# Scatters to expert slots issued from a list, two or three a round, with a fixed GpSimd order, in layer 3's cross attention

## The chip, the cores and the metric

The kernel runs on one core of a Trainium2 chip. A core has five engines that run side by side, each with a queue of instructions of its own which it takes in order: TensorE (PE, matrix products and transposes), VectorE (DVE), ScalarE (ACT), GpSimd (POOL) and SyncE (SP, here only DMA issue). An instruction waits for the work of other engines by semaphores, and whatever stands behind it on its own engine waits too. GpSimd does arithmetic and also issues DMAs, among them the indirect ones that are the subject here.

The metric is the device time of one execution in microseconds (us), less is better.

## The reference

The reference is a decoder of four layers on `x` of 4 batches x 512 tokens x 128 features; each layer adds self attention, cross attention to a context of 77 rows, and a feed-forward part to `x`. What matters here is the end, layer 3's cross attention and its feed-forward part, a mixture of 32 experts with a limited number of slots each:

```python
# cross attention: 16 heads of 64, 77 keys
scores = jnp.einsum('bhqd,bhkd->bhqk', q, k) * scale
attn = jax.nn.softmax(scores, axis=-1)
out = jnp.einsum('bhqk,bhkd->bhqd', attn, v)
...
# feed-forward: every token goes to K = 4 of E = 32 experts, C = 128 slots an expert
scores = jax.nn.sigmoid(logits)
_, idx = jax.lax.top_k(scores + bias[None, :], K)
w = jnp.take_along_axis(scores, idx, axis=-1)
w = w / jnp.clip(jnp.sum(w, axis=-1, keepdims=True), 1e-12, None)
pos = jnp.take_along_axis(jnp.cumsum(onehot, axis=0) - 1, eid[:, None], axis=1)[:, 0]
valid = pos < C
xe = jnp.zeros((E, C, D), x.dtype).at[eid, posc].add(jnp.where(valid[:, None], Xrep, jnp.zeros((), x.dtype)))
h = jax.nn.silu(jnp.einsum('ecd,edi->eci', xe, W1)) * jnp.einsum('ecd,edi->eci', xe, W3)
ye = jnp.einsum('eci,eid->ecd', h, W2)
out = (ye[eid, posc] * gflat[:, None]).reshape(-1, K, D).sum(axis=1)
out = out + jax.nn.silu(X @ sw1.T) * (X @ sw3.T) @ sw2.T
```

A token's slot within an expert is its place in the count over all earlier tokens, so batches are routed one after the other.

## The kernel before

**Rounds of the cross attention.** `l3_xattn` goes through 32 items: four batches of eight pairs of heads. `lagged` makes rounds of four phases: in round r it writes the projection of item r, the scores and softmax of item r-1, the product with the values (`acc`) of item r-4, and the transposes (`turn`) of item r-3. The scores are two score tiles an item; for each, VectorE takes the maximum, subtracts it, ScalarE takes the exponential, VectorE sums and takes the reciprocal, and GpSimd multiplies by it (the multiplication at L2165, tile `heads`). TensorE's transposes of `heads` (L2173) need both multiplications of their item.

**The routing beside it.** When the last item of a batch is summed (`yT`, L2188), `chain5` adds it to `x`, normalizes the tokens and calls `route_slots`: router matmuls, sigmoid, top four, the running counts, and for each token and choice the number of its slot (`to`) and its row with weight and place (`sent`, last written at L784). Then 16 indirect DMAs (L788; four tiles of tokens by four choices, 128 rows each) scatter the rows into the tensor `slots`. GpSimd issues them. Batches 0, 1 and 2 go this way; batch 3 is computed densely at the end, from bf16 copies of the weights (`in_bf16`, six loads that GpSimd issues since they cast).

**Order.** `weave(dense, chain, every)` runs the generator `dense` and takes one step of `chain` for each `every` steps of it; what is left of the chain follows at the end. The first 40 steps of the rounds have the norms of other batches beside them, the next 32 have batch 0's routing, the next 32 batch 1's, and the rest batch 2's. What is written so isn't yet the order of the queues: a scheduler takes the instructions by priority and by its own estimate of when they are ready, and orders every engine's queue. Under `manual_schedule` an engine keeps the order in which its instructions were written; before, only VectorE does so, in the last part. `alone` declares that scatters needn't wait for each other.

**After the rounds.** `slot_experts` fetches the slots of four experts at a time (SP, L837), which needs all scatters done, turns them on TensorE (L842), multiplies with the experts' weights and scatters the results back (L885). `returned` adds them to `x` and stores it. Shared rows and the dense path of batch 3 are woven with it.

The names that the prediction speaks of: `heads` L2165 and L2173, `slots` L788, `sent` L784, `yT` L2188, `kb` (the keys, cleared at L2112), and the loads at L375.

Of the kernel before, what the change touches and what calls it, by code (L numbers as in the profile page):

```python
# [23 lines left out]
B, S, D = 4, 512, 128  # L24
# [14 lines left out]
class Pack:  # L39


    def __init__(self):
        self.parts, self.at, self.n = [], {}, 0
# [248 lines left out]
class Net:  # L292
# [7 lines left out]
    def __init__(self, ctx, tc, packs, dram, feed):  # L300
        self.tc, self.nc = tc, tc.nc
        self.packs, self.dram = packs, dram
        self.feed, self.loaded = feed, []
        self.stay = {}
        self.turn = 0
        self.last = []
        self.chunks, self.sums = {}, {}
        nc = self.nc
        pool = lambda name, bufs, **kw: ctx.enter_context(tc.tile_pool(name=name, bufs=bufs, **kw))
        self.keep = pool("keep", 1)  # L310
        self.wpool = pool("weights", self.SLOTS)
        self.small = pool("small", 4)
        self.away = pool("away", 1, space=bass.MemoryType.DRAM)

        k = self.keep
        self.x = k.tile([P, NT, D], F32, name="x")
        self.xn = k.tile([P, NT, D], F32, name="xn")
        self.xT = k.tile([P, NT * P], F32, name="xT")
        xin = dram["x"].rearrange("(t p) d -> p t d", p=P)
        fetch = lambda b: nc.sync.dma_start(self.x[:, TB * b : TB * b + TB, :], xin[:, TB * b : TB * b + TB, :])  # L320
        fetch(0)
        self.want(0)
        self.const = self.load("const", k, "const")
        self.want(1)
        for b in range(1, B):
            fetch(b)
        self.ident = k.tile([P, P], F32, name="ident")
        make_identity(nc, self.ident)
        self.ones = k.tile([P, P], F32, name="ones")
        nc.gpsimd.memset(self.ones, 1.0)  # L330
        self.identb = k.tile([P, P], BF16, name="identb")
        nc.vector.tensor_copy(self.identb, self.ident)
        self.onesb = k.tile([3, P], BF16, name="onesb")
        nc.gpsimd.memset(self.onesb, 1.0)

        self.causal = k.tile([P, P], BF16, name="causal")
        nc.gpsimd.memset(self.causal, 0.0)
        nc.gpsimd.affine_select(
            out=self.causal, in_=self.causal, pattern=[[-1, P]], compare_op=ALU.is_ge,
            fill=-BIG, base=0, channel_multiplier=1,  # L340
        )
# [3 lines left out]
    def pool(self, name, bufs=1, right=False):  # L345
        return self.tc.tile_pool(
            name=name, bufs=bufs, side="right" if right else "left", reuse_waits="tile"
        )
# [400 lines left out]
    def route_slots(self, b, W, pool):  # L749


        nc = self.nc
        E, K = 32, 4
        m = {}
        one = lambda shape, name: pool.tile(shape, F32, tag=name, name=name, bufs=1)
        own = lambda shape, dt, name: pool.tile(shape, dt, name=f"{name}{b}", bufs=1)
        yield from self.capped(b, W, pool, m)

        code = one([P, TB, E], "code")
        self.tt(code, m["place"], self.const["slot1"].unsqueeze(1).to_broadcast([P, TB, E]), ALU.add)  # L760
        self.tt(code, code, m["fits"], ALU.mult)
        yield
        m8 = one([P, TB, 8], "m8")
        for t in range(TB):
            nc.vector.max(m8[:, t, :], code[:, t, :])
        yield
        top = m8[:, :, :K]
        to, none = own([P, TB, K], I32, "to"), one([P, TB, K], "none")
        nc.vector.tensor_scalar(none, top, 0.0, 2.0 * E * CAP, ALU.is_equal, ALU.mult)
        nc.vector.scalar_tensor_tensor(to, top, -1.0, none, ALU.add, ALU.add)  # L770

        sent = pool.tile([P, TB, K, D + 2], F32, name="sent", tag="sent", bufs=2)
        for t in range(TB):
            nc.scalar.copy(sent[:, t, :, :D], self.xn[:, TB * b + t, :].unsqueeze(1).to_broadcast([P, K, D]))
        nc.vector.tensor_scalar(
            sent[:, :, :, D + 1].bitcast(I32), self.const["place"].rearrange("p (t k) -> p t k", k=K),
            float(b * S * K), None, ALU.add,
        )
        yield
        same = one([P, TB, K, E], "same")  # L780
        wide = lambda a: a.unsqueeze(2).to_broadcast([P, TB, K, E])
        self.tt(same, wide(code), top.unsqueeze(3).to_broadcast([P, TB, K, E]), ALU.is_equal)
        self.tt(same, same, wide(m["w"]), ALU.mult)
        nc.vector.tensor_reduce(sent[:, :, :, D], same, AX.X, ALU.add)  # L784
        for t in range(TB):
            for k in range(K):

                self.alone("slots", nc.gpsimd.indirect_dma_start(  # L788
                    out=self.slots, out_offset=bass.IndirectOffsetOnAxis(ap=to[:, t, k : k + 1], axis=0),
                    in_=sent[:, t, k, :], in_offset=None, bounds_check=E * CAP - 1, oob_is_err=False,  # L790
                ))
                if k % 2:
                    yield

    def alone(self, group, put):

# [1322 lines left out]
    def l3_xattn(self, base, pool):  # L2119
# [3 lines left out]
        nc, tc = self.nc, self.tc  # L2123
# [18 lines left out]
        def scores(b, hp):  # L2142
            q = made.pop((b, hp, "q"))
            es = []
            for j0 in range(0, TB, 2):
                s = self.mm((P, 4, L))
                for j in range(2):
                    self.dot(
                        s[:, 2 * j : 2 * j + 2, :].rearrange("p h l -> p (h l)"),
                        (q[:, (j0 + j) * P : (j0 + j + 1) * P], kb[:, hp, b].rearrange("p h l -> p (h l)")),  # L2150
                    )
                es.append(s)
            if hp == 0:
                made[b, "e"] = pool.tile([P, TB, 16, L], F32, tag="heads", name="heads", bufs=2)
            for i, s in enumerate(es):
                s = s.rearrange("p (j h) l -> p j h l", j=2)
                e = made[b, "e"][:, 2 * i : 2 * i + 2, 2 * hp : 2 * hp + 2, :]
                m, r = (pool.tile([P, 2, 2], F32, tag=t, name=t, bufs=8) for t in ("sm_m", "sm_s"))
                wide = lambda a: a.unsqueeze(3).to_broadcast([P, 2, 2, L])
                nc.vector.tensor_reduce(m, s, AX.X, ALU.max)  # L2160
                self.tt(e, s, wide(m), ALU.subtract)
                nc.scalar.activation(e, e, AF.Exp)
                nc.vector.tensor_reduce(r, e, AX.X, ALU.add)
                nc.vector.reciprocal(r, r)
                nc.gpsimd.tensor_tensor(e, e, wide(r), ALU.mult)  # L2165

        def turn(b, hp):
            e = made[b, "e"].rearrange("p j h l -> p j (h l)")
            for i in blocks[hp]:
                r0, r1 = rows[i]  # L2170
                t = self.mm((P, TB, P))
                for j in range(TB):
                    nc.tensor.transpose(t[: r1 - r0, j, :], e[:, j, r0:r1], self.ident)  # L2173
                eT = pool.tile([P, S], F32, tag="eT", name="eT", bufs=4)
                nc.scalar.copy(eT[: r1 - r0], t[: r1 - r0].rearrange("l j q -> l (j q)"))
                made[b, i] = eT

        def values(b, hp):
# [7 lines left out]
            if hp == HP - 1:  # L2186
                self.sums["l3_xattn", b] = pool.tile([P, S], F32, tag="yT", name="yT", bufs=2)
                nc.scalar.copy(self.sums["l3_xattn", b], accs[b])  # L2188

        return self.lagged(items, (projections, 0), (scores, 1), (values, 4), (turn, 3))  # L2190

    def out(self, b):
# [5 lines left out]
def chained(*chains):  # L2198
    for c in chains:
        yield from c  # L2200


def some(steps, n):

    for _ in range(n):
        if next(steps, steps) is steps:
            return
        yield


def build(nc, packs, dram):
# [4 lines left out]
    at = {}  # L2216
# [6 lines left out]
    with tile.TileContext(nc) as tc, ExitStack() as ctx:  # L2223
        net = Net(ctx, tc, packs, dram, feed)
# [118 lines left out]
        steps = net.l3_xattn(at["x3"], x3)  # L2343
# [5 lines left out]
        def onto_x3(b):  # L2349
            net.add_columns(b, net.sums.pop(("l3_xattn", b)))  # L2350
            yield
            yield from net.norm(b)
# [2 lines left out]
        W5 = Both()  # L2355
        chain5 = lambda b: chained(onto_x3(b), net.route_slots(b, W5, s5))
        net.weave(some(steps, 40), chained(net.norm(1), net.norm(2), net.norm(3)), 3)
        net.weave(some(steps, 32), chain5(0), 1.35)
        net.want(at["l3"] + 1)
        net.weave(some(steps, 32), chain5(1), 1.35)  # L2360
        net.weave(steps, chain5(2), 1.0)
        net.add_columns(3, net.sums.pop(("l3_xattn", 3)))
        close_pool("x3")
        close_pool("x3c")
# [43 lines left out]
```

## Time and profile before

| | us |
|---|---|
| three runs | 2242.82, 2245.49, 2256.26 |
| median | 2245.49 |
| the profiled execution | 2248.78 |
| its span in the trace | 2247.0 |
| mean granted TensorE clock | 0.958 of full |

The trace is of the profiled execution, so sums of its durations stand against 2248.78 and 2247.0, not against the median.

A row of a group of instructions reads: line, engine, operation, what is written <- what is read (buffer numbers left out), shape, count | busy time, mean ns of one | idle time of the engine just ahead of them, and what ended most of it. A row of a timeline reads: start, duration, engine, line, operation, and in brackets the idle time ahead of it and what ended that. Where the stage lies, in times from the span's start:

| event | us |
|---|---|
| first multiplication of `heads` on GpSimd | 1984.78 |
| sums `yT` of batches 0, 1, 2, 3 copied | 2015.56, 2049.10, 2095.98, 2141.48 |
| first scatter of batches 0, 1, 2 | 2047.71, 2093.93, 2138.26 |
| last scatter begins | 2157.58 |
| slots fetched, first issue | 2159.73 |
| first scatter back | 2179.67 |

One scatter takes GpSimd 966 to 1132 ns (median 972), and lands a median 2.1 us after its issue.

### The profile page before, as it was taken

The numbers are of one execution on the slowest core, as the hardware profiler recorded it, in microseconds if no ns is written. First come the engines' busy times: TensorE is split into PE (matmuls) and PEld (weight loads), VectorE is DVE, ScalarE is ACT, GpSimd is POOL, SyncE is SP. The second block draws the span as 40 slices with busy tenths as digits, with TensorE's granted clock in tenths as the row PEclk, the third lists the DMA queues.
The fourth block names the chain that finished last, engine by engine and source line by source line (L and its number), as shares of the span: only waits on it lengthen the run. The fifth ranks groups of instructions, "written<-read, shape, count | busy, mean of one in ns | idle before, by whom it ended". The sixth has DMA issues, their size and how long they took to land.

```text
span 2247.0 us, 28205 instructions
## 1 busy us (share of the span) xinstructions
PE 2100.3 (93%) x8974; PEld 1112.3 (50%) x8980; DVE 1608.4 (72%) x4061; ACT 998.2 (44%) x2044; POOL 555.1 (25%) x695
## 2 busy tenths in 40 slices
PE   6999899999999999999999999999999999498897
PEld 3556556645544554445444544444444444365553
DVE  6676575566675769778977797877787775687745
ACT  3665546443325543534543353444444443255532
POOL 1000000000000000433433333333333331335544
PEclk8999899999999999999999999999999999799888
DMA  6321135154353342433433444443443444200032
GB/s 168 94 72 44 46 102 133 54 134 128 98 147 89 89 116 83 98 95 91 110 104 100 112 124 122 122 113 97 124 110 100 104 112 106 94 2 6 10 94 78
DMA packets 89811, 214.93 MB, mean 96 GB/s; under 512 B 21970, under 2 KB 40850, under 8 KB 89406
## 3 DMA queue, kind: packets, MB, share of 16 engines
q1 hardware_dynamic: 86094, 209.20, 35.5%
q0 software_dynamic: 3568, 3.93, 0.6%
q8 instruction: 71, 1.16, 0.2%
q14 instruction: 78, 0.64, 0.1%
HBM read 184.00 MB, written 23.53 MB: 92 GB/s over the span
## 4 chain that ended last, share of the span: by engine, by line
PE 72%; DVE 17%; issue 4%; ACT 3%; POOL 2%; DMA 2%; SPq 0%; DVEq 0%; ACTq 0%; POOLq 0%
PE mm L425 19%; PE f L425 13%; PE s L425 8%; PE mm L1873 8%; PE acc L1032 6%; PE mm L1845 5%; PE mm L1820 4%; DVE h L436 2%; PE mm L1200 1%; PE mm L1155 1%; PE mm L1222 1%; DVE m L1162 1%; DVE at_m L1902 1%; PE acc L2183 1%; PE s L515 1%
## 5 line engine op out<-in xcount | busy, mean ns | idle before, releaser
L1781 POOL TENSOR_TENSOR gvx<-gvx 128x512 f32<-128x512 f32 (+1 forms) x256 | 260.6, 1018 | 550.5 <-DVE gvx L436 481.9
L425 PE MATMUL f<-xT,w_l_ffn 128*128 128x512 f32 (+1 forms) x700 | 338.4, 605 | 1.2 <-ACT h L1024 0.7
L1904 ACT ACTIVATE at_e<-mm,at_m 128x512 f32<-128x512 f32 x256 | 173.0, 685 | 294.2 <-DVE at_m L1902 275.4
L425 PE MATMUL mm<-w_l_ffn_qkv,xT 128*128 128x512 f32 x512 | 267.0, 606 | 4.2 <-ACT at_e L1904 1.8
L1873 PE MATMUL mm<-og,w_l_ffn_o 128*128 128x512 f32 x512 | 265.6, 603 | 3.2 <-DVE og L436 3.2
L436 DVE TENSOR_TENSOR h<-h,f 128x512 f32<-128x512 f32 (+1 forms) x192 | 131.3, 685 | 132.8 <-PE f L425 107.7
L1024 ACT ACTIVATE h<-f 128x512 f32<-128x512 f32 x189 | 112.4, 596 | 233.9 <-PE f L425 201.9
L1032 PE MATMUL acc<-h,w_l_ffn 128*128 128x512 f32 x378 | 196.9, 605 | 4.7 <-DVE h L436 4.1
L425 PEld LDWEIGHTS f<-xT,w_l_ffn 128*128 128x128 f32 (+1 forms) x700 | 126.9, 192 | 132.9 <-issue 111.2
L436 DVE TENSOR_TENSOR gvx<-mm,gv 128x512 f32<-128x512 f32 x256 | 174.8, 685 | 22.2 <-PE mm L425 18.6
L436 DVE TENSOR_TENSOR og<-mm,c 128x512 f32<-128x512 f32 x256 | 176.7, 692 | 18.0 <-PE mm L1873 15.9
L1821 ACT COPY eT<-mm 128x512 f32<-128x512 f32 x256 | 137.6, 596 | 83.4 <-PE mm L1820 83.2
L1902 DVE TENSOR_REDUCE at_m<-mm 128x1 f32<-128x512 f32 x256 | 161.3, 683 | 12.0 <-PE mm L425 10.6
L1820 PEld LDWEIGHTS mm<-ident,at_e 128*128 128x128 f32 x1024 | 120.7, 142 | 68.2 <-issue 47.9
L1873 PEld LDWEIGHTS mm<-og,w_l_ffn_o 128*128 128x128 f32 x512 | 91.7, 191 | 114.4 <-issue 90.0
L1820 PE MATMUL mm<-ident,at_e 128*128 128x128 f32 x1024 | 135.9, 275 | 5.3 <-ACT at_e L1904 5.3
L425 PEld LDWEIGHTS mm<-w_l_ffn_qkv,xT 128*128 128x128 f32 x512 | 87.6, 191 | 95.1 <-issue 59.2
L425 PE MATMUL mm<-roped 64*128 64x512 f32 x512 | 130.9, 623 | 1.7 <-DVE roped L436 1.0
L1162 DVE TENSOR_REDUCE m<-mm 128x1 f32<-128x512 f32 (+3 forms) x176 | 105.2, 637 | 32.7 <-PE mm L1158 31.8
L1845 PE MATMUL mm<-eT,v 128*64 128x512 f32 x512 | 118.6, 599 | 0.0
L1032 PEld LDWEIGHTS acc<-h,w_l_ffn 128*128 128x128 f32 x378 | 71.2, 193 | 90.2 <-issue 59.9
L436 DVE TENSOR_TENSOR h<-h,c 128x512 f32<-128x512 f32 x160 | 110.5, 697 | 3.9 <-DMA c<-l_ffn_w 1.1
(458 smaller groups left out, 3556.1 us busy)
## 6 DMA issues: line engine op xcount, KB each, us to landing
c<-gates SPq DMA_DIRECT2D x256, 256.0 KB
c<-l_ffn_w SPq DMA_DIRECT2D x96, 384.0 KB
w_l_ffn<-in_l_ffn SPq DMA_DIRECT2D x26, 576.0 KB
w_l_ffn_qkv<-in_l_ffn_qkv SPq DMA_DIRECT2D x16, 640.0 KB
w_l_ffn_o<-in_l_ffn_o SPq DMA_DIRECT2D x16, 512.0 KB
rot<-qk SPq DMA_DIRECT2D x128, 64.0 KB
d<-inverted SPq DMA_DIRECT2D x64, 128.0 KB
k_parts<-k SPq DMA_DIRECT2D x12, 384.0 KB
```

The source lines that it names most:

```text
L425: self.nc.tensor.matmul(out, lhsT=lhsT, rhs=rhs, start=i == 0, stop=i == len(pairs) - 1)
L436: self.nc.vector.tensor_tensor(out, a, b, op)
L1024: nc.scalar.activation(h, pg, AF.Silu)
L1032: nc.tensor.matmul(acc["t"], lhsT=W["d" + u], rhs=h, start=i == 0, stop=i == n - 1)
L1162: nc.vector.tensor_reduce(m[:, i, h0 : h0 + per], ps, AX.X, ALU.max, negate=True)
L1781: nc.gpsimd.tensor_tensor(x[:, :, :m], x[:, :, :m], x[:, :, m : 2 * m], ALU.add)
L1820: nc.tensor.transpose(p[:, j, :], es[i][hl][:, j * P : j * P + P], self.ident)
L1821: nc.scalar.copy(eT[hl][:, :, i * P : i * P + P], p)
L1845: nc.tensor.matmul(po[64 * hl : 64 * hl + 64, :], lhsT=m["v"][:, j, hl, :], rhs=eT[hl][:, j, :], start=j == 0, stop=j == TB - 1,)
L1873: nc.tensor.matmul(acc, lhsT=W["o"][:, (e - 1) * D : e * D], rhs=hs.pop(e - 1), start=e == 1, stop=e == E)
L1902: nc.vector.tensor_reduce(m, s, AX.X, ALU.max, negate=True)
L1904: nc.scalar.activation(e[:, :n], s, AF.Exp, bias=m, accum_out=den)
```

## The change

The scatters are no longer issued where `route_slots` makes their rows. It puts them on a list, `puts`, and the round's own `scores` issues from the list at its end, two a round, three in the rounds of the last batch. The three weaves with routing stand under `manual_schedule` for GpSimd, so that its queue keeps the order as written, and what is left on the list is issued after them. The weaves' third argument goes from 1.35, 1.35, 1.0 to 1.7, 1.7, 1.2; `route_slots` yields once in place of eight times at its end.

```diff
@@ -303,6 +303,7 @@
         self.turn = 0
+        self.puts = []
         self.last = []
@@ -785,12 +786,16 @@
         for t in range(TB):
             for k in range(K):
 
-                self.alone("slots", nc.gpsimd.indirect_dma_start(
+                self.puts.append(lambda t=t, k=k: self.alone("slots", nc.gpsimd.indirect_dma_start(
                     out=self.slots, out_offset=bass.IndirectOffsetOnAxis(ap=to[:, t, k : k + 1], axis=0),
                     in_=sent[:, t, k, :], in_offset=None, bounds_check=E * CAP - 1, oob_is_err=False,
-                ))
-                if k % 2:
-                    yield
+                )))
+        yield
+
+    def put(self, n):
+
+        for _ in range(min(n, len(self.puts))):
+            self.puts.pop(0)()
@@ -2163,6 +2168,7 @@
                 nc.vector.reciprocal(r, r)
                 nc.gpsimd.tensor_tensor(e, e, wide(r), ALU.mult)
+            self.put(3 if b == B - 1 else 2)
@@ -2355,10 +2361,12 @@
         net.weave(some(steps, 40), chained(net.norm(1), net.norm(2), net.norm(3)), 3)
-        net.weave(some(steps, 32), chain5(0), 1.35)
-        net.want(at["l3"] + 1)
-        net.weave(some(steps, 32), chain5(1), 1.35)
-        net.weave(steps, chain5(2), 1.0)
+        with tc.manual_schedule(engines={mybir.EngineType.Pool}):
+            net.weave(some(steps, 32), chain5(0), 1.7)
+            net.want(at["l3"] + 1)
+            net.weave(some(steps, 32), chain5(1), 1.7)
+            net.weave(steps, chain5(2), 1.2)
+            net.put(len(net.puts))
         net.add_columns(3, net.sums.pop(("l3_xattn", 3)))
```

The same instructions remain on every engine, and the sync queue keeps its order. GpSimd's order in the two programs, through the cross attention (m: a round's two multiplications, s: a scatter, L: a bf16 weight load at L375, z: the clearing of a router's padding):

```
before: 30m' z 4m' 6s m' 2s m' 4s 2m' 4s 8m' z 4m' 6s m' 2s m' 4s 2m' 4s 8m' z 2m' 16s LLL   (m': one multiplication)
after:  14m z 5m 2s LL m 2s L m 2s m 2s z m 2s m 2s m 3s m 1s m 3s m 3s m 3s z m 3s m 3s z m 17s LLL
```

The three loads among the first scatters stood at 1840.09, 1872.64 and 1885.98 us before.

## The prediction

> **What bounds the kernel now.** First the page's totals, to see which engine carries the kernel.
>
> ```profile
> span 2247.0 us, 28205 instructions
> PE 2100.3 (93%) x8974; PEld 1112.3 (50%) x8980; DVE 1608.4 (72%) x4061; ACT 998.2 (44%) x2044; POOL 555.1 (25%) x695
> ```
>
> TensorE is busy 93% of the span, so a change elsewhere pays only where TensorE waits. The change touches one stage, layer 3's cross attention with the routing of batches 0 to 2, about 1976 to 2158 us. The second view is busy time by stretches of it (columns: TensorE, weight loads, VectorE, ScalarE, GpSimd, granted clock, DMA share, GB/s).
>
> ```profile
> 2020.00:2040.00 20.00, 19.03 (x106) 13.34 (x105) 17.43 (x80) 15.33 (x31) 6.45 (x11) 1.00 0.00 1
> 2040.00:2060.00 20.00, 14.14 (x69) 9.42 (x69) 12.93 (x42) 7.04 (x15) 12.39 (x14) 0.90 0.05 14
> 2060.00:2080.00 20.00, 16.28 (x66) 10.57 (x65) 12.65 (x50) 8.72 (x20) 13.20 (x17) 0.84 0.02 1
> 2080.00:2100.00 20.00, 19.50 (x104) 13.44 (x102) 18.83 (x75) 14.76 (x28) 8.98 (x12) 1.00 0.01 2
> 2100.00:2120.00 20.00, 12.39 (x38) 7.25 (x39) 8.88 (x36) 4.72 (x10) 16.28 (x20) 0.77 0.01 0
> 2120.00:2140.00 20.00, 17.38 (x81) 11.94 (x80) 14.31 (x63) 12.59 (x24) 6.13 (x9) 0.81 0.08 26
> ```
>
> Until 2040 TensorE never rests and its clock is full. Then come two dents, 2040 to 2080 and 2100 to 2120, and in exactly these GpSimd is busiest. The groups of instructions on TensorE in 1984 to 2140 (the tail of a row is the idle time ahead of it) name the wait:
>
> ```profile
> L2173 PE MATMUL mm<-ident,heads 128*128 128x128 f32 x144 | 24.8, 288 | 18.1 <-POOL heads L2165 18.1
> ```
>
> The timelines of GpSimd and of TensorE show why:
>
> ```profile
> 2046.60 0.70 POOL L2165 TENSOR_TENSOR heads<-heads,sm_s 128x308 f32<-128x308 f32 x1 [0.78 <-DVE sm_s L2164]
> 2047.71 1.13 POOL L788 DMA_INDIRECT slots<-sent,to  x1 [0.41 <-DVE sent L784]
> 2049.15 1.00 POOL L788 DMA_INDIRECT slots<-sent,to  x1 [0.30 <-issue]
> ...
> 2055.27 0.72 POOL L2165 TENSOR_TENSOR heads<-heads,sm_s 128x308 f32<-128x308 f32 x1
> ...
> 2136.83 0.99 POOL L2165 TENSOR_TENSOR heads<-heads,sm_s 128x308 f32<-128x308 f32 x1 [0.94 <-DVE sm_s L2164]
> ...
> 2157.58 0.97 POOL L788 DMA_INDIRECT slots<-sent,to  x1 [0.30 <-issue]
> ```
>
> ```profile
> 2056.05 0.69 PE L2173 MATMUL mm<-ident,heads 128*128 128x128 f32 x2 [3.35 <-POOL heads L2165]
> 2059.25 0.69 PE L2173 MATMUL mm<-ident,heads 128*128 128x128 f32 x2 [2.51 <-POOL heads L2165]
> 2071.37 0.44 PE L2173 MATMUL mm<-ident,heads 128*128 128x128 f32 x2 [2.53 <-POOL heads L2165]
> 2073.18 2.26 PE L425 MATMUL mm<-kb,q 128*128 128x154 f32 x8
> ```
>
> A batch's 16 scatters follow each other every 1.275 us, six of them before the next heads multiplication. The softmax of that round had long been finished (its reciprocal ran at 2049.25, the multiplication at 2055.27), TensorE stood for the transposes, and afterwards ran at half speed: the eight score matmuls took 2.26 us at 2073.18 where they take 1.21 at 2023.50.
>
> **The change, part by part.** (a) *The fixed order on GpSimd.* The changed program's order has 38 multiplications (rounds 0 to 18, two each), then two scatters after every round; three from batch 3's first round on, one where batch 0's list runs out. Seventeen stand behind the last multiplication (one of batch 1, all of batch 2); before it was sixteen.
>
> When does this stretch begin? Round 18's last reciprocal is at 2052.96 in VectorE's timeline, plus 0.17, plus the multiplication's 0.70: about 2053.9. (Before, batch 0's first six scatters ran in the meantime, 2047.7 to 2055.3, which now come later.) Up to the last multiplication GpSimd then has 31 scatters x 1.275 = 39.5 us; 26 multiplications x 0.70 plus a 0.17 us start after each group of scatters, 13 times = 20.4; memsets 0.4; and the three weight loads of (b) 1.8. Sum 62.1 us, so the last multiplication ends near 2116.0, against 2136.83 + 0.99 = 2137.8 before: 21.8 us earlier. Seventeen scatters x 1.275 = 21.7 end at 2137.7, against 2157.58 + 0.97 = 2158.55: 20.9 us earlier. The gain is GpSimd's idle time: in the 110.8 us from its first to its last scatter it had 48 x 1.275 + 30 x 0.72 + 0.5 = 83 us of work and some 28 us idle, because its scatters were used up in a block and it then waited for VectorE.
>
> Can the others follow? TensorE: a round takes 3.2 us in the undisturbed part (acc matmuls at 2018.14, 2021.34, 2024.55), with the ten blocks for eight rounds about 3.5; 13 rounds 46 us, plus the routing matmuls and transposes of two batches, 3.7 us each (yT and xn transposes 0.44 each, gates 0.92, eight pairs of counts 1.9): 53 us of the 62. In rounds with two scatters GpSimd (4.1 us) and TensorE (3.5 + about 0.5 of routing) are level; with three (5.4 us) TensorE idles 1.9 us a round. VectorE: the four softmax instructions of half a round occupy 1.23 us from start to start (0.38 three times and 0.09), 2.5 us a round, 30 us for the 12 rounds left, plus 11 us for each routing sequence: at most 52 of 62. Scores run two rounds ahead of the transposes, so a hiccup of 1 or 2 us in either doesn't reach GpSimd.
>
> What is queued behind what: behind each scatter stands the next round's multiplication, for which TensorE's transposes wait, then eT, acc, and the third batch's sum. In the order built, a batch's first scatter comes behind a multiplication whose softmax lies on VectorE after the weights that it sends (`sent`), so batches 0 and 1 should not hold GpSimd; only batch 2's first scatter waits for VectorE by itself. Batch 2's sum was copied at 2095.98; now its last multiplication (round 23) is due 22 us after 2053.9, at 2076, and turn, copy, scores and acc add 4.5: 2080. From copy to `sent` the sequence took 31.8 us for batch 0 (2015.56 to 2047.4, undisturbed), 44.5 and 42 for the two that were held up. With 32 it ends at 2112, with 42 at 2122, against 2116 when GpSimd asks. I take the first, as the hold-ups go, and keep up to 6 us as a loss.
>
> (b) *Three bf16 weight loads* (for packs 0 to 2 of the last stage) leave the GpSimd queue at 1840.1, 1872.6 and 1886.0 and come between the first scatters. They took 0.86, 0.57 and 0.59 us: 1.8 counted above (1.7 to 2.6). Where they leave, GpSimd was waiting anyway (29.0 us at 1872.6, behind which only the clearing of `kb` stood, which is not read before 1976), so nothing is gained; a loss or gain there is bounded by the 4.2 us of that memset. They land in a median 4.8 us, are needed some 110 us later, and the eighth DMA after each, which shares its semaphore, is over 10 us behind. Nothing.
>
> (c) *The weave* (1.7, 1.7, 1.2 in place of 1.35, 1.35, 1.0) moves matmuls, VectorE and ScalarE instructions by a few places; a sequence has seven fewer steps, so it still ends inside its 32 steps. The memset for the routers and the order on the sync queue: SP's order is the same, instruction by instruction. Zero, with 4 us either way for order effects.
>
> (d) *After the last multiplication.* Turn, acc and sum of batch 3, its norm and routing, and the shared rows fill 2137.8 to 2172.5, where the first slots are turned with no wait. This is moved whole: the fetch of slots waits for the last scatter (2159.73 after 2158.55), 20.9 us earlier, TensorE's part 21.8 earlier; some 3 to 5 us of slack lie between landing and use. The rest to the end has the same order.
>
> Sum: 21 us less, about 2226 of the 2247.0 span, 2227.8 of that execution's 2248.78. That execution is 3.3 us above the median 2245.49, so the median becomes 2224.5; I state 2225.
>
> **Two rules weighed.** The row: gaps of 3.35 and 2.51 us, and one of 2.53, were enough for half speed for some 3.4 us after. The Trainium skill ("TensorE: Matmul & The Clock Gate", Part 1) says that the clock falls after an idle window of about 3.4 us and returns after a busy one. By the rule the new gaps of at most 1.9 us cost nothing; by the row they are near enough to fear. If each of six rounds lost 1.7 us so, the 10 us would lie in the 1.9 x 6 = 11 us TensorE has spare. I take nothing, and keep 10 for the range. Against this change speaks "SBUF — State Buffer" (SBUF: two separate sides): VectorE in a two-port mode shuts GpSimd out from writing DMA descriptors, and scatters now lie beside more VectorE work. The row: the scatters at 2093.93 to 2100.36, with VectorE busy throughout, are 1.275 us apart, as at 2140 and later with it mostly free. The measurement decides: no surcharge; by the rule even 0.3 us on 31 scatters would take 9 us of the gain.
>
> **Rivals.** *The routing sequence decides* (batch 2 late, 42 us or more): scatters end near 2144, less slack 3, a gain of 12 to 16: 2231. For it: VectorE at 52 of 62 us. Against: its two slow passes both contained a GpSimd hold-up. *More than the sum*: the tail's TensorE work ran at half speed from 2131 to 2165 after gaps; starting it warm would give 4 to 8 more: 2218. *Slower*: TensorE's clock. In rounds 19 to 31 the 53 us of TensorE work take 106 if the clock stays at half through regular small gaps; last multiplication at 2160, 22 us late: 2267. It decides from a mean granted clock of 53 / 83.9 = 0.63 downwards. Against: the worst slice shown before was 0.77, and a slowed TensorE leaves no gap. *The change does nothing it says*: excluded by the order on GpSimd as built.
>
> **How the numbers follow.** Forecast (gain 17 to 25) 0.53; routing sequence (8 to 17) 0.20; more than the sum (over 25) 0.10; part of the gain eaten by clock or order, within 8 us of zero, 0.08; slower 0.09. One per cent, about what a measurement of this kernel tells from no change, is 22.5 us, so three eighths of the forecast's case and all of "more" lie beyond: faster by over 1% 0.30, within 1% 0.61, slower by over 1% 0.09. Range 2214 to 2240: it leaves out the slower case and the tip of the other.
>
> **What would show it.** Right: scatters in twos and threes between multiplications, GpSimd over 90% busy from about 2054 to 2116, TensorE's wait for `heads` at L2173 spread in gaps under 2 us, the last multiplication near 2116, the last scatter near 2138, the same 89 us from there to the end. Wrong: GpSimd waiting for `sent` ahead of a scatter, a granted clock under 0.7 in this stretch, or slots that TensorE waits for.

## The result and the profile after

| | before | after |
|---|---|---|
| median | 2247.07 us (4 runs, 2242.82 to 2256.26) | 2222.62 us (4 runs, 2218.29 to 2230.94) |
| the profiled execution | 2248.78 | 2226.72 |
| its span in the trace | 2247.0 | 2224.9 |

The ratio is 0.9889, 95% interval 0.9861 to 0.9917: 24.5 us by the medians, 22.1 by the spans of the two traces. The forecast was 2225.0 us and a gain of 21. The median before now includes a fourth run beside the three shown above. By the medians the gain is 1.1%, just over the one per cent for which the prediction gave 0.30; the interval reaches to both sides of it.

In the profile after, the lines of the code have moved by five or six: the multiplication of `heads` is now L2170, the transposes L2179, `acc` L2189, `yT` L2194, the scatters L789. First the page's totals:

```profile
span 2224.9 us, 28180 instructions
PE 2092.9 (94%) x8974; PEld 1108.7 (50%) x8980; DVE 1606.7 (72%) x4061; ACT 998.2 (45%) x2044; POOL 556.1 (25%) x695
```

No engine has less work: GpSimd is busy 556.1 us where it was 555.1, VectorE 1606.7 where it was 1608.4. TensorE runs as many matmuls as before, in 2092.9 us instead of 2100.3, since less of them falls into half speed (mean granted clock 0.962 against 0.958), and it idles 132.0 us instead of 146.7. So about two thirds of the 22.1 us came out of its waiting and one third out of the clock that fell with the waits. TensorE's share rises from 93% to 94%. By stretches of the changed stage (busy time of TensorE, weight loads, VectorE, ScalarE, GpSimd, then granted clock, DMA share, GB/s):

```profile
2020.00:2040.00 20.00, 19.25 (x105) 13.46 (x104) 17.04 (x73) 14.99 (x30) 6.12 (x10) 1.00 0.00 1
2040.00:2060.00 20.00, 19.82 (x103) 13.57 (x101) 19.11 (x70) 12.13 (x25) 11.64 (x15) 1.00 0.20 60
2060.00:2080.00 20.00, 18.92 (x104) 13.16 (x104) 18.31 (x75) 15.26 (x30) 17.30 (x23) 1.00 0.13 35
2080.00:2100.00 20.00, 18.16 (x92) 11.92 (x91) 17.91 (x67) 11.03 (x24) 15.90 (x19) 1.00 0.02 1
2100.00:2120.00 20.00, 14.49 (x54) 9.09 (x54) 11.03 (x51) 10.25 (x19) 15.53 (x20) 0.74 0.09 24
2120.00:2140.00 20.00, 16.71 (x47) 7.83 (x46) 10.02 (x43) 8.99 (x14) 14.35 (x16) 0.66 0.33 103
```

The dent of 2040 to 2080 is gone: TensorE is busy 38.7 of those 40 us (30.4 before) at full clock (0.90 and 0.84 before), and GpSimd's work, which stood in two blocks with rests between, is spread over 2050 to 2137. What stays is a dent at 2100 to 2140, with the clock at 0.74 and 0.66. The group of transposes that waited 18.1 us for `heads` in 1984 to 2140:

```profile
L2179 PE MATMUL mm<-ident,heads 128*128 128x128 f32 x144 | 24.4, 284 | 7.3 <-POOL heads L2170 7.3
```

GpSimd's timeline shows the new order, and TensorE's what is left of the waits:

```profile
2050.58 1.36 POOL L2170 TENSOR_TENSOR heads<-heads,sm_s 128x308 f32<-128x308 f32 x2 [2.05 <-DVE sm_s L2169]
2052.12 1.14 POOL L789 DMA_INDIRECT slots<-sent,to  x1 [0.18 <-issue]
2053.56 0.98 POOL L789 DMA_INDIRECT slots<-sent,to  x1 [0.30 <-DVE st L484]
2054.52 1.19 POOL L376 DMA_DIRECT2D w_l_ffn<-in_l_ffn  x2
2055.66 1.44 POOL L2170 TENSOR_TENSOR heads<-heads,sm_s 128x308 f32<-128x308 f32 x2
...
2112.67 0.70 POOL L2170 TENSOR_TENSOR heads<-heads,sm_s 128x308 f32<-128x308 f32 x1 [0.99 <-DVE sm_s L2169]
2113.53 1.35 POOL L789 DMA_INDIRECT slots<-sent,to  x1 [0.15 <-issue]
2115.72 0.97 POOL L789 DMA_INDIRECT slots<-sent,to  x1 [0.84 <-DVE sent L785]
```

```profile
2091.19 0.44 PE L2179 MATMUL mm<-ident,heads 128*128 128x128 f32 x2 [0.17 <-POOL heads L2170]
...
2096.29 0.44 PE L2179 MATMUL mm<-ident,heads 128*128 128x128 f32 x2 [1.25 <-POOL heads L2170]
...
2101.45 0.44 PE L2179 MATMUL mm<-ident,heads 128*128 128x128 f32 x2 [0.38 <-POOL heads L2170]
...
2106.57 1.34 PE L2179 MATMUL mm<-ident,heads 128*128 128x128 f32 x4 [3.21 <-POOL heads L2170]
```

From 2052 to 2113 GpSimd rests only 0.64, 0.90 and 0.99 us at a time, apart from the 0.30 between two scatters and 0.15 to 0.18 behind a multiplication. Its last multiplication ends at 2113.37 (2137.8 before), the last scatter at 2136.31 (2158.55), the first slots are turned at 2150.37 (2172.49). Of the gaps that used to stand in the second and the third batch's rounds 0.66 us is the longest that is left. In the last batch's rounds, with three scatters, the four gaps shown follow, and the fourth, 3.21 us, is the one after which four transposes take 1.34 us instead of 0.60.

### The profile page after: what moved, and what is told of

Read it like the earlier page. It is cut to its first block, busy times and chain, and to the rows that moved or that the text cites. A ratio compares the mean times of both kernels' runs of the same rounds, so it can differ in the third digit from the quotient of the medians.

```text
span 2224.9 us, 28180 instructions
## 1 busy us (share of the span) xinstructions
PE 2092.9 (94%) x8974; PEld 1108.7 (50%) x8980; DVE 1606.7 (72%) x4061; ACT 998.2 (45%) x2044; POOL 556.1 (25%) x695
## 4 chain that ended last, share of the span: by engine, by line
PE 74%; DVE 16%; issue 4%; ACT 3%; DMA 2%; POOL 2%; SPq 0%; DVEq 0%; POOLq 0%; ACTq 0%
PE mm L426 20%; PE f L426 13%; PE mm L1878 8%; PE s L426 8%; PE acc L1037 6%; PE mm L1850 5%; PE mm L1825 4%; DVE h L437 2%; PE mm L1160 1%; PE mm L1227 1%; PE mm L1205 1%; PE acc L2189 1%; DVE at_m L1907 1%; DVE m L1167 1%; PE s L516 1%
## 5 line engine op out<-in xcount | busy, mean ns | idle before, releaser
L1825 PEld LDWEIGHTS mm<-ident,at_e 128*128 128x128 f32 x1024 | 120.9, 142 | 68.0 <-issue 47.5
L1825 PE MATMUL mm<-ident,at_e 128*128 128x128 f32 x1024 | 136.4, 275 | 5.3 <-ACT at_e L1909 5.3
L1850 PE MATMUL mm<-eT,v 128*64 128x512 f32 x512 | 118.6, 599 | 0.0
```

The costliest lines, as they stand in the source:

```text
L1825: nc.tensor.transpose(p[:, j, :], es[i][hl][:, j * P : j * P + P], self.ident)
L1850: nc.tensor.matmul(po[64 * hl : 64 * hl + 64, :], lhsT=m["v"][:, j, hl, :], rhs=eT[hl][:, j, :], start=j == 0, stop=j == TB - 1,)
```

## The experiments

Three groups of four kernels ran on three chips, on which the kernel before takes 2257.65, 2259.92 and 2245.36 us. So ratios to the kernel before on the same chip are compared. Times inside the profiles are given from the copy of batch 0's sum (`yT`, the last event that all share before the first scatter); what lies ahead of it differed by some microseconds between executions of even the same kernel (2011.34 to 2013.99 us from the start for the changed one).

| kernel | ratio (95%) | last multiplication ends | last scatter ends | first slots turned | wait for `heads` |
|---|---|---|---|---|---|
| before | 1 | 122.3 | 143.0 | 156.9 | 18.1 |
| after | 0.9889 (0.9861 to 0.9917) | 99.4 | 122.3 | 136.4 | 7.3 |
| e1 list and weaves only | 0.9999 (0.9978 to 1.0019) | 118.6 | 141.1 | 160.3 | 17.9 |
| e2 fixed order only | 1.0022 (1.0009 to 1.0036) | 126.3 | 144.0 | 163.6 | 19.7 |
| e3 old weave numbers | 0.9913 (0.9887 to 0.9938) | 107.9 | 128.9 | 146.5 | 10.9 |
| e4 two a round | 0.9919 (0.9894 to 0.9944) | 96.2 | 124.5 | 144.1 | 2.2 |
| e5 the changed kernel | 0.9903 (0.9880 to 0.9926) | 99.3 | 121.8 | 142.9 | 7.1 |
| e6 two a round | 0.9908 (0.9883 to 0.9933) | 96.2 | 124.9 | 145.6 | 2.2 |
| e7 sixteen at once | 1.0031 (1.0018 to 1.0045) | 127.0 | 150.1 | 169.9 | 26.4 |
| e8 half on VectorE | 0.9895 (0.9871 to 0.9919) | 95.0 | 120.9 | 142.3 | 2.5 |
| e9 the changed kernel | 0.9896 (0.9868 to 0.9925) | 99.3 | 121.8 | 133.0 | 7.1 |
| e10 one a round | 0.9961 (0.9940 to 0.9982) | 92.5 | 138.3 | 145.8 | 0.2 |
| e11 without batch 2's scatters | 0.9903 (0.9878 to 0.9928) | 99.3 | 100.8 (the one left) | 132.8 | 7.2 |
| e12 without batch 0's and 1's | 0.9908 (0.9883 to 0.9933) | 95.0 | 118.7 | 130.3 | 0.0 |

The last column is TensorE's wait for GpSimd's `heads` in the stage. In e8 the last multiplication on GpSimd is meant; half of the last batch's are on VectorE.

### Which part carries the gain: e1, e2, e7

The theory: the gain is made by scatters that stand two or three at a time between the multiplications. The rivals: the list and the weave, or the fixed order by itself. e1 takes the fixed order away:

```diff
-        with tc.manual_schedule(engines={mybir.EngineType.Pool}):
+        if True:
```

> The changed kernel with its list, its puts in the rounds and its new weaves, but without the fixed order on GpSimd, so that the scheduler orders that queue again (as built: batches of 1 and 5, 1 and 3, 2 and 4 scatters between single multiplications, then 8 in a row, as in the kernel before). Theory (the gain is GpSimd's order: scatters spread two or three a round under it): the gain goes, 2240 to 2248 us, TensorE waits for heads 15 us or more in 1984 to 2140, last multiplication of heads near 2137. Rival (the list and the new weaves carry the gain, the order is only kept): 2220 to 2226 us. Between, near 2232, both would have a share.

Measured: 0.9999. The list and the new weave numbers, without the order, bring nothing. The scheduler took the puts out of their places again, as GpSimd's timeline of e1 shows:

```profile
2059.96 0.73 POOL L2170 TENSOR_TENSOR heads<-heads,sm_s 128x308 f32<-128x308 f32 x1
2060.86 1.03 POOL L789 DMA_INDIRECT slots<-sent,to  x1 [0.18 <-issue]
2062.19 0.98 POOL L789 DMA_INDIRECT slots<-sent,to  x1 [0.30 <-DVE sm_m L2165]
2063.47 0.97 POOL L789 DMA_INDIRECT slots<-sent,to  x1 [0.30 <-issue]
2064.75 0.97 POOL L789 DMA_INDIRECT slots<-sent,to  x1 [0.30 <-issue]
2066.03 0.97 POOL L789 DMA_INDIRECT slots<-sent,to  x1 [0.30 <-DVE sm_m L2165]
2067.01 0.72 POOL L2170 TENSOR_TENSOR heads<-heads,sm_s 128x308 f32<-128x308 f32 x1
```

Five scatters stand between a round's two multiplications, which are 7.05 us apart, as in the kernel before; TensorE's wait is 17.9 us.

e2 is the other half: the kernel before with GpSimd's order fixed as written, and nothing else.

```diff
-        net.weave(some(steps, 32), chain5(0), 1.35)
...
+        with tc.manual_schedule(engines={mybir.EngineType.Pool}):
+            net.weave(some(steps, 32), chain5(0), 1.35)
...
```

> The kernel before with GpSimd's order fixed as written in the three weaves and nothing else: six scatters, two multiplications, six scatters, two multiplications, four scatters for batches 0 and 1, and 14 behind the last multiplication. Theory (spreading is what counts, a fixed order with blocks of six still leaves 7.7 us between two rounds' multiplications where TensorE has 3.5 us of work a round): TensorE's waits for heads 12 us or more, granted clock falling below 0.9 in those stretches, 2236 to 2247 us. Rival (what cost was the scheduler's splitting of a round's two multiplications by scatters, so any fixed order mends it): 2220 to 2228 us.

Measured: 1.0022, a little slower than before. The fixed order moves the three weight loads too (it puts them behind batch 0's scatters), and with that move in it the run gains nothing. What was written before the change were blocks of six, six and four, and TensorE's timeline has a gap for each:

```profile
2058.34 1.34 PE L2173 MATMUL mm<-ident,heads 128*128 128x128 f32 x4 [3.26 <-POOL heads L2165]
2067.27 0.44 PE L2173 MATMUL mm<-ident,heads 128*128 128x128 f32 x2 [3.64 <-POOL heads L2165]
...
2074.79 0.44 PE L2173 MATMUL mm<-ident,heads 128*128 128x128 f32 x2 [1.99 <-POOL heads L2165]
```

e7 keeps everything of the change, list, order, weaves and the loads' places, and takes only the spreading away:

```diff
-            self.put(3 if b == B - 1 else 2)
+            self.put(16)
```

> The changed kernel with all 16 scatters of a batch issued in the first round after its rows are made: list, fixed order, weaves and the loads' places stay, only the spreading goes. Theory (spreading is the whole gain): GpSimd stays away from heads for 20.4 us twice, TensorE waits for heads 20 to 30 us in 1984 to 2140 and falls to half speed in both blocks; last multiplication near 2137 or later, ratio to the kernel before 0.998 to 1.010. Rival (what counts is that fewer scatters stand behind the last multiplication or that the order is fixed): 0.986 to 0.993.

Measured: 1.0031, inside the theory's 0.998 to 1.010. The last multiplication comes 27.7 us later than in the changed kernel (127.0 against 99.3), and the gaps stand where the blocks are, one of 11.55 us behind batch 0's rows and this one behind batch 1's:

```profile
2125.45 0.69 PE L2179 MATMUL mm<-ident,heads 128*128 128x128 f32 x2 [14.82 <-POOL heads L2170]
```

So spreading under a fixed order is what carries the gain; neither half does it alone. This is shown, on two chips.

### The weave numbers: e3

```diff
-            net.weave(some(steps, 32), chain5(0), 1.7)
+            net.weave(some(steps, 32), chain5(0), 1.35)
-            net.weave(some(steps, 32), chain5(1), 1.7)
+            net.weave(some(steps, 32), chain5(1), 1.35)
-            net.weave(steps, chain5(2), 1.2)
+            net.weave(steps, chain5(2), 1.0)
```

> The changed kernel with the weaves' third arguments back at 1.35, 1.35, 1.0. The first scatters come one round sooner in GpSimd's order, and 16 in place of 17 stand behind the last multiplication. Theory (the weave numbers are worth nothing, term c): 2219 to 2226 us, last multiplication of heads within 3 us of 2113. Rival (the later, thinner weave keeps the routing's VectorE and TensorE work out of the rounds' way and carries a good part of the gain): 2231 us or more.

The ratio, 0.9913, keeps most of the gain, so the rival (2231 us or more, 0.993 or above) falls by its point value, though the interval reaches to 0.9938. But the last multiplication comes at 107.9, 8.6 us behind the control's 99.3, where within 3 us was expected. VectorE's and GpSimd's timelines of e3 name what is late:

```profile
2116.74 0.29 DVE L715 SCALAR_TENSOR_TENSOR fits<-s,chosen 128x128 f32<-128x128 f32 x1 [6.95 <-PE s L426]
```

```profile
2118.70 0.70 POOL L2170 TENSOR_TENSOR heads<-heads,sm_s 128x308 f32<-128x308 f32 x1 [6.39 <-DVE sm_s L2169]
```

With the old numbers batch 2's routing falls so that its comparison `fits`, which needs TensorE's counts, stands on VectorE ahead of the last round's softmax. VectorE waits 6.95 us for the counts, the softmax behind it is late, and GpSimd, whose next instruction is the multiplication for that softmax, stands still 6.39 us. At the first slots 3.6 us of the 8.6 are left (146.5 against 142.9 in e5, on a different chip of about the same speed). So the new numbers have a share, at most some 4 us of the end, that the ratios can't separate from nothing.

### More or less spreading: e4, e6, e8, with e5 as control

```diff
-            self.put(3 if b == B - 1 else 2)
+            self.put(2)
```

> The changed kernel with two scatters in every round, also in batch 3's: 22 instead of 17 stand behind the last multiplication. GpSimd has five scatters, 6.4 us, less ahead of it. Theory (GpSimd with three scatters a round holds TensorE back in batch 3's rounds, and the tail behind is set by TensorE): last multiplication near 2107 (2113.4 in the changed kernel), last scatter as there, near 2136, since batch 2's rows are ready only near 2115; the 3.2 us gap on TensorE ahead of half speed goes; first slots turned 2144 to 2147; 2214 to 2219 us. Rival (the tail is set by the last scatter and the slots' landing): first slots turned near 2150 behind a wait for slots, 2221 to 2225 us.

The first part came out by half: the last multiplication is 3.2 us sooner (96.2 against 99.4) where 6.4 was expected, the last scatter 2.2 us later, TensorE waits for `heads` 2.2 us instead of 7.3, and the 3.2 us gap is gone, though not the half speed (see the clock, below). The second part did not: the first slots were turned at 144.1, 7.7 us later than in the profile after, with no wait for slots there, so neither side's account of the tail was right. The same kernel and the changed one then ran side by side:

> The changed kernel as it is, as the control beside the next three on the same chip. Both theories: a ratio to the kernel before of 0.986 to 0.992; last multiplication of heads some 61 us after round 18's last one, last scatter some 23 us behind it.

> Two scatters in every round, beside the control. In its first profile the last multiplication came 5 us sooner than in the changed kernel, but the first slots were turned 6.6 us later, behind stalls of 3.5 and 1.75 us of TensorE that no engine's row explains and a wait of 4.6 us for batch 3's own routing. Theory A (those stalls belong to that chip, as the other three profiles taken there have them too, and TensorE's earlier start is worth 4 to 6 us): a ratio 0.002 to 0.003 below the control's. Theory B (the last scatter, which stays near 2136, sets the end): the control's ratio within 0.001.

The control gave 0.9903 and two a round 0.9908: Theory B's number, but not its mechanism, since no wait for slots stands ahead of the first slots in e6 either. Batch 3's sum was copied 3.6 us sooner than in the control (101.6 against 105.2 after batch 0's), and the first slots came 2.7 us later: the earlier start was lost in the tail. In the control, too, the tail is longer here than on the chip of the profile after: 43.6 us from the last multiplication to the first slots, against 37.0. TensorE's and ScalarE's timelines of e5 show where:

```profile
2134.39 1.91 PE L426 MATMUL s<-w_s_gate,xT 128*128 128x32 f32 x8 [6.12 <-issue]
```

```profile
2130.20 0.59 ACT L920 ACTIVATE h<-f 64x512 f32<-64x512 f32 x1 [5.63 <-remote]
2133.75 0.58 ACT L517 COPY xT<-s 128x512 f32<-128x512 f32 x1 [2.97 <-remote]
```

The 6.12 us ahead of batch 3's gate matmuls are put down to nothing ("issue"), and in the profile after there is no such gap. But the gate reads `xT`, and ScalarE ends the copy to it at 2134.33, just ahead of the gate. ScalarE itself had stood twice, for 5.63 and 2.97 us, put down to something that the profile doesn't show ("remote"): TensorE had ended the `f` that it reads at 2126.65, 3.5 us before ScalarE took it up, and in e9, below, it follows at once. So the stall stands on ScalarE first and TensorE waits behind it. In the eight profiles of the first two chips the sigmoid behind the gate began 19.5 to 26.2 us after batch 3's sum (15.7 in e2), in the profiles before and after 14.7 and 14.8. e1, e2 and e7, which gain nothing, are among the eight, so these stalls don't tell before from after. In six of the eight the sigmoid began 3.4 to 4.2 us after the last scatter's start, which suggested that the scatters hold it.

e8 takes 5.6 us of multiplications off GpSimd:

```diff
-                nc.gpsimd.tensor_tensor(e, e, wide(r), ALU.mult)
+                (nc.vector if b == B - 1 and i else nc.gpsimd).tensor_tensor(e, e, wide(r), ALU.mult)
```

> The changed kernel with the second of the two multiplications of batch 3's eight rounds on VectorE instead of GpSimd. GpSimd loses 8 x 0.70 = 5.6 us ahead of the last multiplication, VectorE gains about 8 x 0.38 = 3 us. Theory (GpSimd is the bound up to the last multiplication): it comes 4 to 6 us sooner against the control, TensorE's waits for heads in that stretch shrink from 7 us to below 4, ratio 0.0015 to 0.003 below the control's where TensorE sets the tail. Rival (VectorE or the third batch's routing is as tight as GpSimd there): last multiplication within 2 us of the control's, the third batch's rows later, ratio equal to the control's or above.

GpSimd's last multiplication comes 4.3 us sooner and TensorE's waits for GpSimd shrink to 2.5 us (1.2 more are for VectorE): GpSimd was the bound there. But the last scatter is only 0.9 us sooner, because GpSimd now waits for batch 2's rows:

```profile
2108.69 0.97 POOL L789 DMA_INDIRECT slots<-sent,to  x1 [4.58 <-DVE sent L785]
```

0.9895 against the control's 0.9903 lies within both intervals. It isn't shown to beat the changed kernel.

### What is left to win, and what the tail hangs on: e10, e11, e12, with e9 as control

> The changed kernel again, as the control of the next three. A ratio to the kernel before of 0.988 to 0.993; from the copy of batch 3's sum to the first slots turned 37 to 38 us if this chip is like the second and third, 31 if it is like the first.

0.9896, and 27.8 us from batch 3's sum to the first slots: this chip is free of the stalls.

```diff
-            self.put(3 if b == B - 1 else 2)
+            self.put(1)
```

> One scatter a round, so that 35 stand behind the last multiplication of heads instead of 17. GpSimd has 18 x 1.275 = 23 us less ahead of it, and no longer holds TensorE. Theory A (TensorE's work sets the end): last multiplication 8 to 10 us sooner than in the control, near the 53 us behind round 18 that TensorE needs; ratio 0.002 or more below the control's. Theory B (the last scatter sets the end, through the slots or through whatever holds batch 3's sigmoid until it): last scatter 10 to 13 us later than in the control, first slots turned as much later, ratio 0.994 to 0.997.

The last multiplication comes 6.8 us sooner, less than the 8 to 10 expected, and the last scatter 16.5 us later, where 10 to 13 were expected; the first slots are turned 12.9 us later. The ratio 0.9961 is Theory B's. TensorE's timeline of e10:

```profile
2142.15 1.02 PE L1037 MATMUL acc<-h,w_l_ffn 128*128 128x512 f32 x2
2159.21 1.11 PE L847 MATMUL f<-ident,slots 128*128 128x128 f32 x4 [16.05 <-DMA slots<-slots]
```

TensorE is through with all it has by 2143.17 and stands 16.05 us for the slots, which come 7.5 us after the last scatter ends at 2151.68. In the control the first slots are turned 11.2 us after the last scatter's end. So the control has 11.2 - 7.5 = 3.7 us of slack there, and 16.5 less 3.7 is the delay of the first slots: what goes beyond the slack is paid in full.

e11 leaves out the scatters of batch 2:

```diff
+                if b == 2:
+                    continue
                 self.puts.append(lambda t=t, k=k: self.alone("slots", nc.gpsimd.indirect_dma_start(
```

> The changed kernel with the 16 scatters of batch 2 left out (its rows never reach the slots), so that one scatter stands behind the last multiplication instead of 17; everything ahead is as in the control. Theory (the 6 to 8 us for which batch 3's norm and routing stood on the second and third chip belong to the scatters that run beside them: the sigmoid of batch 3 began 3.4 to 4.2 us after the last scatter's start in six of eight profiles there): the sigmoid begins 14 to 16 us after batch 3's sum is copied, the first slots are turned 30 to 32 us after it, ratio 0.003 below the control's. Rival (they come from something else): the sigmoid 19 to 20 us, the slots 37 to 38 us after the sum, ratio within 0.001 of the control's.

The first slots are turned 132.8 after batch 0's sum, against 133.0 in the control, and the ratios agree: the 16 scatters behind the last multiplication cost nothing that this measurement shows on this chip. Of the stalls it says nothing, since the control here has none (its sigmoid began 13.3 us after batch 3's sum, that of e11 13.1). Whether the scatters cause them on the other two chips stays open.

e12 leaves out those of batches 0 and 1 (`if b < 2` in place of `if b == 2`):

> The changed kernel with the 32 scatters of batches 0 and 1 left out (their rows never reach the slots), so that GpSimd has 39.5 us less in the stage and only batch 2's 16 stand at the end. It bounds what any order of the scatters can bring. Theory (GpSimd is the bound up to the last multiplication, TensorE the next at 53 us): last multiplication 8 to 10 us sooner than in the control, TensorE's waits for heads below 2 us, the granted clock full until 2100; last scatter 3 to 7 us sooner, set by batch 2's rows; ratio 0.002 to 0.004 below the control's. Rival (TensorE or VectorE is already the bound): last multiplication within 3 us of the control's, same ratio.

With 32 scatters gone from the stage, 31 of them (39.5 us of GpSimd) ahead of the last multiplication, this comes 4.3 us sooner, not 8 to 10, and the first slots 2.7 us sooner; TensorE's wait for `heads` is zero. The ratio, 0.9908, isn't below the control's. So the changed kernel already hides nearly all that these scatters cost. It isn't the limit for the last multiplication, which e10 has at 92.5, sooner than the 95.0 here. Batch 3's sum, which TensorE makes behind it, comes 5.9 us sooner than in the control in e12 and 6.4 in e10. So some 6 us are left ahead of that sum, where GpSimd no longer holds TensorE, and no ratio here shows that any of it reaches the end.

## Why the prediction was right, step by step

- **The mechanism.** GpSimd's blocks made TensorE wait, and spreading them fills GpSimd's rests. Confirmed: without spreading (e7) or without the order that keeps it (e1) the gain is gone. Counted from batch 0's sum the last multiplication comes 22.9 us sooner, where 21.8 was forecast, and the first slots 20.5, where 21 was. That the end agrees so closely is in part luck: the stretch came out a little better than the sum, and 2.1 us were lost behind it (see the clock).
- **Where the stretch begins.** Forecast 2053.9; round 18's last multiplication ended at 2050.58 + 1.36 = 2051.94. In this execution batch 0's sum, ahead of everything changed, was already 1.6 us early, which is within what executions of one kernel differ by.
- **The 62.1 us of GpSimd's work.** Measured 2113.37 - 2051.94 = 61.4. The last scatter was due 21.7 us behind the last multiplication and ended 22.9 behind it: some 0.5 of the 1.2 us more is the wait for batch 2's rows (0.84 where 0.30 is usual), and two of the scatters took 1.35 and 1.44 us. Batch 2's sum was due at 2080 and was copied at 2081.01. Its routing took 34 us (2081.01 to 2115.4) where 32 was taken and 42 feared; GpSimd asked at 2114.9. So the rival in which the routing decides was close: the rows came some 0.5 us too late here, and in e8 GpSimd stood 4.58 us for them.
- **TensorE's gaps in rounds with three scatters.** The estimate of 1.9 us a round was too simple. The gaps were 0.17, 1.25, 0.38 and 3.21 us; that work written ahead swallowed most of the first three and then ran out is an inference. TensorE's 53 us of work were about right: with GpSimd out of the way by one scatter a round (e10) the last multiplication comes 6.9 us sooner than in the profile after, 61.4 - 6.9 = 54.5 behind round 18.
- **The clock.** Taken at no cost, with half speed feared from 1.9 us gaps. In the profile after, gaps of 1.25 us and less left the clock full, and half speed followed the one of 3.21 us, from 2105.8 to 2116.0. The Trainium skill ("TensorE: Matmul & The Clock Gate", Part 1) gives about 3.4 us of idleness as enough. Two rows speak against using that as a bound. In e3 a gap of 1.17 us, the third of its kind in 12 us, was followed by four transposes at 1.34 us. In e4, without the 3.2 us gap, half speed came all the same and stayed as long, after gaps of 0.51 and 0.70 us:

```profile
2097.90:2101.30 3.40, 2.02 (x15) 1.44 (x13) 2.42 (x9) 3.35 (x6) 3.07 (x4) 1.00 0.19 66
2101.30:2111.50 10.20, 8.80 (x28) 6.21 (x29) 7.77 (x42) 3.78 (x7) 5.50 (x7) 0.50 0.02 3
```

  In both, eight small gate matmuls (128x32) stand just ahead; whether these, the short gaps or both did it is not shown. Behind the last multiplication TensorE still had `acc` matmuls to do, at half speed (3.57 us for four at 2112.64, where four at 2117.11 took 1.99), so that batch 3's sum was copied 5.8 us behind it (5.9 in e5 and e9), and 3.7 before. These 2.1 us are what the prediction left out here; how much of them is the clock and how much work that had piled up isn't separated. The slower rival needed a mean clock of 0.63 over the stage, and the stage had 1.00, 1.00 and 0.74.
- **No surcharge for scatters beside VectorE's work.** With VectorE busy 18.3 of 20 us, scatters at 2077.23, 2078.54 and 2079.82 start 1.31 and 1.28 us apart. No surcharge showed; whether VectorE was in a two-port mode there no trace tells, so the rule itself was not tested.
- **The loads, part (b).** No gain, as e2 has them moved without one. They landed in 3.8 us before; the 4.8 that was read is that of three later loads, which changes nothing.
- **The weave, part (c).** Taken at zero. This is the term that was mis-sized: the old numbers cost 8.6 us at the last multiplication (e3), by a wait of VectorE that the prediction had not looked for, and some 3.6 us of it reach the slots. It stayed inside the 4 us that had been kept for it. The sum came out without it because it was worked out for the order with the new numbers.
- **The tail, part (d).** Moved nearly whole: the slack of 3 to 5 us that was read off measures 3.7 (e10 and e9). The 89 us from last scatter to end became 2224.9 - 2136.3 = 88.6. From the last multiplication on, 109.2 us became 111.5, and 2.1 of the 2.3 are those ahead of batch 3's sum; from that sum to the first slots it was 31.0 us before and 31.2 after. The rival *more than the sum* read half speed from 2131 to 2165 in the profile before. There TensorE was at full clock in between, with gaps, and fell again behind batch 3's sum:

```profile
2131.00:2138.00 7.00, 7.00 (x17) 3.97 (x16) 4.72 (x18) 1.88 (x5) 1.69 (x2) 0.51 0.01 2
2138.00:2148.00 10.00, 5.98 (x23) 2.66 (x22) 4.46 (x22) 3.79 (x6) 7.61 (x8) 1.00 0.37 118
```

So the tail's half speed follows a gap of its own behind batch 3's sum (3.05 us before, 3.29 after), and an earlier, warmer start doesn't take it away: it begins 6.7 us behind the sum before and 7.1 after, and lasts 13.7 us in both.

## What to carry to other kernels

When an engine that is idle half of the stage is nevertheless waited for, look at the order on its queue before its load: short work that the critical engine needs must not stand behind a block of work that nobody needs yet. Putting the pieces where they belong in the code is not enough where a scheduler reorders the queue, and pinning the order is not enough where the code writes them in a block; here it took both. How many pieces to place in a round follows from two limits, the rest the engine has in a round and the slack at the far end, and on either side of the right number (one, or sixteen) the loss is much larger than between neighbours (two or three).

## What the runs showed of the hardware that was not expected

**Half speed lasts differently long in the same program.** The changed kernel's profile and that of e9, the same kernel in another execution, come to batch 3's norm with gaps of 3.29 and 3.17 us on TensorE, and go on with the same matmuls. First the profile after, then e9, by stretches of 4 us (columns as above):

```profile
2126.00:2130.00 4.00, 4.00 (x13) 1.61 (x11) 0.69 (x1) 1.69 (x5) 3.08 (x4) 0.53 0.02 0
2130.00:2134.00 4.00, 4.00 (x12) 2.22 (x11) 1.31 (x2) 2.71 (x5) 3.15 (x3) 0.50 0.02 0
2134.00:2138.00 4.00, 4.00 (x11) 2.38 (x12) 1.95 (x8) 2.17 (x4) 3.63 (x5) 0.50 0.15 27
```

```profile
2122.00:2126.00 4.00, 3.05 (x12) 1.55 (x12) 1.60 (x4) 1.65 (x4) 3.08 (x4) 0.74 0.03 4
2126.00:2130.00 4.00, 4.00 (x19) 2.18 (x19) 1.28 (x2) 3.17 (x5) 3.09 (x4) 0.84 0.02 0
2130.00:2134.00 4.00, 2.62 (x11) 1.03 (x11) 3.33 (x18) 2.57 (x4) 3.39 (x5) 1.00 0.02 1
```

In the first TensorE is busy without a break and still at half speed for some 13 us; in the second it is back within about 4. The other profile of an unstalled tail with the same order ahead of it, e11, is like e9, and the kernel before is like the profile after. From the last multiplication to the first slots this makes 37.0 against 33.6 us. A single profile is therefore worth some 3 us less or more in such a tail.

**The same program stands still on some chips and not on others.** On two chips batch 3's sigmoid began 19.5 to 26.2 us after its sum (15.7 in e2), on the third and in the two first profiles 13.1 to 14.8. The changed kernel needs 43.6 us from the last multiplication to the first slots in e5 and 33.6 in e9. In e5 the stall stands on ScalarE first, and no releaser of it is in the trace. The kernel before is slower on those two chips too, by 12 to 15 us against the third. The cause wasn't found.
